# Softmax denominators of both halves of the heads in one tile, turned once for 512 queries

## The chip, the core and the metric

The kernel runs on one core of one Trainium2 chip. The metric is the time on the device in microseconds. Before the change it was 3248.77 us, the median of three runs (3247.61 to 3251.02).

## The reference

A graph attention layer with residuals and layer norms works on 8 frames of 2048 nodes with 256 channels each. There are 8 heads of 32 channels. All data are fp32. The adjacency matrix is the same for all frames.

```python
qkv = jnp.einsum('fnc,ck->fnk', x, w_qkv)
scores = jnp.einsum('fnhd,fmhd->fhnm', q, k) / jnp.sqrt(jnp.asarray(D, x.dtype))
scores = jnp.where(mask, scores, jnp.asarray(-1000000000.0, x.dtype))
attn = jax.nn.softmax(scores, axis=-1)
t = jnp.einsum('fhnm,fmhd->fnhd', attn, v).reshape(F, N, C)
x = _layernorm(x + t, ln1_g, ln1_b)
h = jax.nn.relu(jnp.einsum('fnc,cd->fnd', x, w1) + b1)
f_out = jnp.einsum('fnd,dc->fnc', h, w2) + b2
x = _layernorm(x + f_out, ln2_g, ln2_b)
```

Around it stands one more residual and norm: the output is the layer norm of the input plus this layer's result. The kernel doesn't subtract a maximum before the exponential. It computes exponentials, sums them for each head and query (the denominators), and divides at the end. It also keeps a running sum and minimum of the denominators (RS); if they are out of range, another, slower path recomputes everything. That path isn't taken here.

## The kernel before

**Tiles and items.** The queries of a frame are cut in 4 chunks of 512 (qc), the heads in 2 halves of 4 (g), the keys in 16 blocks of 128 (mb). An item is (frame, qc, g, mb). There are 8 x 4 x 2 x 16 = 1024 items, 128 to a frame, and the main loop (L552) goes through them in this order. Scores are computed with keys on the partitions and queries along the free dimension: an item is a tile p of 128 keys by 4 heads by 512 queries.

**What an item does.** Four matmuls on TensorE, in different rows of its array, make the scores in two PSUM pairs of banks (L230). VectorE (DVE) adds the mask to each pair and writes it into p (L233). ScalarE (ACT) takes the exponential of p in place (L237). TensorE multiplies with the values into a PSUM bank that holds for all 16 blocks (L249). Scores are two items ahead of the values, exponentials one. The three score pairs rotate, so that scores of an item need that the first mask add of the item before it is done.

**Denominators.** Sums over the keys are first made elementwise over the 16 blocks of a group (f, qc, g). GpSimd (POOL) adds seven of them (POOLED, L271), two chains of four are added by DMAs that accumulate (MOVED, L268, issued on POOL's queue), and one stays alone. That leaves four terms. `denominator` multiplies each with 32 columns of ones, for each head into the 32 partitions of this head (L310), so that a PSUM bank holds the sum of each head, 32 times over, for 512 queries. ACT copies it to dT (L312). TensorE turns dT by four 128x128 transposes (L95, in `transposes`), and DVE takes the reciprocals of one column in 32 into rc (L321) and updates RS (L322, L323). It does this twice for each chunk of queries, once for each half of the heads.

**What follows for a chunk.** After the second half `outcome` starts: `divide` turns the two value tiles oT, DVE multiplies by rc (L345), and a DMA adds the input (L334). `tail` normalizes (`norm`: DVE statistics L278 and L279, four small POOL steps L282 to L286, ACT's L289), goes through the feed-forward (`feed_forward`: L409 to L436, with POOL's L412 and L414), normalizes, scales on POOL (L355, L357), adds the input by a DMA (L359), normalizes again, and stores.

**What sets the order.** The engines work through their own queues in the order in which the program writes them, and a planner in the program writes this order. Besides the main loop there is a list `fill` of generators: denominators, outcomes, tails, and the projections and turned inputs of the next frame (`NEXT`, L499). Once an item, `advance` lets them write some work, ordered by due time. A `yield` tells what a generator needs: a number is a pause in items, BANK the one PSUM bank that the fillers share, MORE the right to another unit in the same bank, WAIT a wait until an item. TensorE's filling is limited by credit: 2200 for each item, not saved up, of which a unit of four 512-column matmuls takes 2048 and a set of four transposes 1400 (TURN). Another unit starts only with 1024 left, or when the filler is overdue. These lines decide it:

```python
state["credit"] = min(max(state["credit"], 0) + STEP, KEPT)
...
return finish or state["credit"] >= UNIT or min(due) <= t
```

A denominator is started two items after its group ends and is due six items after that; its last term waits until the fourth item after the group's end. What the fillers write on DVE, ACT and POOL in an item stands ahead of the mask adds, the exponential and the pool add that the main loop writes next.

## Time and profile before

One execution was profiled. It took 3242.05 us, 6.7 less than the median of the three runs; its span, from the first to the last instruction, is 3240.0 us, at a mean granted TensorE clock of 0.987.

| Engine | busy, us | share of the span |
|---|---|---|
| TensorE matmuls (PE) | 3101.0 | 96% |
| VectorE (DVE) | 2739.5 | 85% |
| GpSimd (POOL) | 2593.3 | 80% |
| ScalarE (ACT) | 2435.5 | 75% |

The costliest groups are DVE's mask adds (2410.5 us), ACT's exponentials (1956.3), POOL's adds (1829.5), and TensorE's scores (1171.2), values (1092.9) and denominators (261.1 for the terms, 47.3 for the turns of dT).

A group's line of the profile gives the source line, engine, operation, output and inputs with their shapes, and the count; then the busy time and the mean duration of one in ns; then how long the engine idled just before them, and what ended that. A timeline's line gives start and duration in us, engine, line, operation, tiles, count, and in brackets the idle time before it with what ended it. TensorE carries out an fp32 matmul as two records, so four matmuls are eight. Records of one engine can overlap: the next begins before the last one's end is written. The chain that ended last goes back from the last instruction to whatever released each step.

### The profile page before, as it was taken

The page shows a single profiled execution, that of the slowest core. Times are in us where ns is not written, and L with a number is a line of the kernel's source. Part 1 is how long each engine was busy: PE and PEld are TensorE (multiplying, and loading weights), DVE is VectorE, ACT ScalarE, POOL GpSimd, SP SyncE. Part 2 cuts the span into 40 slices and gives each one's busy share as a digit, 9 for nine tenths or more (in the row PEclk, how much of TensorE's full clock was granted, in tenths as well). Part 3 has the DMA queues.
Part 4 walks back from the last instruction along what each step waited for, and adds up shares of the span by engine and source line. Part 5 has one row for each costly group of instructions (what it writes and reads, how often), then busy time and mean ns, then how long its engine had stood idle before and what let it go on. Part 6 is the DMA issues. An engine that isn't in the chain of part 4 may idle for free.

```text
span 3240.0 us, 68306 instructions
## 1 busy us (share of the span) xinstructions
PE 3101.0 (96%) x28948; PEld 976.0 (30%) x28948; DVE 2739.5 (85%) x3203; ACT 2435.5 (75%) x1937; POOL 2593.3 (80%) x1357
## 2 busy tenths in 40 slices
PE   7899999999999999999999999999999999998994
PEld 4222333323332233322333323323233323332221
DVE  4888888888888888888988888888888888888994
ACT  3667778778778777778777778777778777777773
POOL 0568888788878888788887888888888788878894
PEclk8899999999999999999999999999999999999997
DMA  9688779778879788788788879878788878877773
GB/s 322 147 179 190 182 175 202 176 174 200 181 176 205 171 190 193 158 195 200 177 181 175 184 181 220 177 167 197 175 192 194 180 171 201 181 171 160 168 160 78
DMA packets 153384, 591.57 MB, mean 183 GB/s; under 512 B 15056, under 2 KB 67792, under 8 KB 103920
## 3 DMA queue, kind: packets, MB, share of 16 engines
q0 software_dynamic: 64560, 435.85, 67.2%
q1 hardware_dynamic: 87696, 149.98, 13.1%
q8 instruction: 229, 3.75, 0.4%
q10 hardware_dynamic: 816, 1.31, 0.1%
q14 instruction: 83, 0.68, 0.1%
HBM read 146.67 MB, written 37.75 MB: 57 GB/s over the span
## 4 chain that ended last, share of the span: by engine, by line
PE 75%; DVE 8%; POOL 5%; DMA 4%; issue 4%; ACT 2%; DVEq 0%; ACTq 0%; POOLq 0%
PE s L230 28%; PE x L249 24%; PE x L54 13%; DVE p L233 6%; PE x L310 6%; PE x L95 4%; DMA p<-p 3%; POOL p L271 2%; ACT p L237 2%; DMA mask<-md 1%; POOL y L357 1%; DVE st L278 1%; POOL y L355 0%; POOL y L414 0%; POOL y L412 0%
## 5 line engine op out<-in xcount | busy, mean ns | idle before, releaser
L233 DVE TENSOR_TENSOR p<-s,mask 128x1024 f32<-128x1024 f32 x2048 | 2410.5, 1219 | 360.3 <-PE s L230 202.9
L237 ACT ACTIVATE p<-p 128x2048 f32<-128x2048 f32 x1024 | 1956.3, 1910 | 510.2 <-DVE p L233 456.7
L271 POOL TENSOR_TENSOR p<-p 128x2048 f32<-128x2048 f32 x382 | 1829.5, 4791 | 216.0 <-ACT p L237 213.8
L230 PE MATMUL s<-qT,kT 32*128 32x512 f32 x8192 | 1171.2, 641 | 34.1 <-DVE p L233 29.1
L249 PE MATMUL x<-p,v 128*32 128x512 f32 x8192 | 1092.9, 606 | 16.7 <-ACT p L237 16.7
L268 POOL DMA_DIRECT2D p<-p x384 | 360.1, 957 | 305.5 <-ACT p L237 95.5
L230 PEld LDWEIGHTS s<-qT,kT 32*128 32x128 f32 x8192 | 320.5, 183 | 637.8 <-DVE p L233 580.1
L249 PEld LDWEIGHTS x<-p,v 128*32 128x32 f32 x8192 | 161.3, 108 | 796.4 <-issue 302.6
L310 PE MATMUL x<-p,ones 128*32 128x512 f32 x2016 | 261.1, 594 | 15.9 <-POOL p L271 9.7
L289 ACT ACTIVATE y<-y,nb,rs 128x256 f32<-128x256 f32 x372 | 219.2, 590 | 46.1 <-POOL nb L286 46.1
L54 PE MATMUL x<-in,wqkv 128*32 128x512 f32 x1888 | 243.5, 592 | 0.0
L278 DVE BATCH_NORM_STATS2 st<-y 128x6 f32<-128x256 f32 x372 | 155.2, 417 | 6.2 <-DMA y<-in_x_dram 6.2
L54 PE MATMUL x<-w2s,hT 128*32 128x256 f32 x2048 | 122.8, 381 | 3.3 <-DVE y L436 2.3
L54 PE MATMUL x<-turned,w1s 128*32 128x512 f32 x992 | 122.9, 592 | 0.4 <-ACT in L166 0.4
L54 PEld LDWEIGHTS x<-wqkv,in 128*32 128x32 f32 x3584 | 102.2, 110 | 63.5 <-issue 59.0
L54 PE MATMUL x<-wqkv,in 128*32 128x128 f32 x3584 | 117.2, 273 | 0.0
L310 PEld LDWEIGHTS x<-p,ones 128*32 128x32 f32 x2016 | 64.1, 110 | 171.4 <-issue 136.0
L54 PEld LDWEIGHTS x<-in,wqkv 128*32 128x32 f32 x1888 | 61.7, 110 | 140.9 <-issue 113.7
L283 POOL TENSOR_TENSOR rs<-rs,mhalf 128x4 f32<-128x4 f32 x93 | 97.1, 1044 | 7.7
L54 PEld LDWEIGHTS x<-w2s,hT 128*32 128x32 f32 x2048 | 66.1, 110 | 76.5 <-issue 30.3
L414 POOL TENSOR_TENSOR y<-y,be1b2r 128x1024 f32<-128x1024 f32 x32 | 85.4, 2667 | 0.6
L355 POOL TENSOR_TENSOR y<-y,g2r 128x1024 f32<-128x1024 f32 x31 | 82.7, 2668 | 1.2 <-ACT y L289 1.2
(117 smaller groups left out, 1333.1 us busy)
## 6 DMA issues: line engine op xcount, KB each, us to landing
p<-p POOLq DMA_DIRECT2D x384, 1024.0 KB, 10.5
in<-xd SPq DMA_DIRECT2D x87, 512.0 KB, 10.7
mask<-md SPq DMA_DIRECT2D x248, 128.0 KB, 8.0
y<-in_x_dram POOLq DMA_DIRECT2D x62, 512.0 KB, 8.0
p<-in_adj_dram SPq DMA_DIRECT2D x16, 1024.0 KB, 9.7
out_dram<-y SPq DMA_DIRECT2D x31, 512.0 KB, 6.4
in<-in_x_dram SPq DMA_DIRECT2D x29, 512.0 KB, 15.9
xd<-in SPq DMA_DIRECT2D x28, 512.0 KB, 10.9
```

The lines of the kernel that those rows point to most:

```text
L54: nc.tensor.matmul(out[r:r + D], lhsT[:, r:r + D], rhs, start=start, stop=stop)
L95: nc.tensor.transpose(ps[:, j * P:(j + 1) * P], s, ident)
L230: nc.tensor.matmul(ps2[half][:, j, :], KT[f, mb // TPC, g][r:r + D, (mb % TPC) * P:(mb % TPC + 1) * P], QT[f, qc, g][r:r + D, :], start=Tr ...
L233: nc.vector.tensor_tensor(pt[:, 2 * half:2 * half + 2, :], ps, MK[f, qc, mb // 2][:, mb % 2, None, :].to_broadcast([P, 2, CH]), ALU.add)
L237: nc.scalar.activation(PT[item], PT[item], AF.Exp, scale=1.0 / math.sqrt(D))
L249: nc.tensor.matmul(O[grp][r:r + D, :], V[f, mb // TPC, g][:, mb % TPC, r:r + D], PT[item][:, h, :], start=(mb == 0), stop=(mb == LAST))
L268: nc.gpsimd.dma_start(PT[f, qc, g, chain[0]], PT.pop(item), accum_op=ALU.add)
L271: nc.gpsimd.tensor_tensor(first, first, PT.pop(item), ALU.add)
L278: nc.vector.bn_stats(st, t[:, j, :])
L283: nc.gpsimd.tensor_tensor(rs, rs, cst["mhalf"], ALU.pow)
L289: nc.scalar.activation(t[:, j, :], t[:, j, :], AF.Identity, bias=nb[:, j:j + 1], scale=rs[:, j:j + 1])
L310: nc.tensor.matmul(ps[r:r + D, :], cst["ones"], term[:, h, :], start=(n == 0), stop=(n == len(terms) - 1))
```

## The change

Instead of 32 columns of ones, the weights of the terms now have ones in only half of the 32 columns: the first 16 for the first half of the heads, the last 16 for the second. The other columns are zero. The first half's sums are copied to dT by ACT as before, and its denominator ends there. The second half's sums are added to dT by DVE, straight from PSUM. The tile then holds, for each position of a head in its half, 16 partitions of the first half's sum and 16 of the second's, and is turned once. The reciprocal takes one column in 16, for all 8 heads; rc now has the halves alternating, and `divide` reads it with a step of two. RS has twice the width. Three memsets make the new weights.

```diff
             for h in range(4):
                 r = D * h
-                nc.tensor.matmul(ps[r:r + D, :], cst["ones"], term[:, h, :], start=(n == 0), stop=(n == len(terms) - 1))
-        dT = op.tile([P, CH], F32, name="dT")
-        nc.scalar.copy(dT, ps)
+                nc.tensor.matmul(ps[r:r + D, :], cst["halves"][:, g, :], term[:, h, :], start=(n == 0), stop=(n == len(terms) - 1))
+        if g == 0:
+            DT[f, qc] = op.tile([P, CH], F32, name="dT")
+            nc.scalar.copy(DT[f, qc], ps)
+            return
+        dT = DT.pop((f, qc))
+        nc.vector.tensor_tensor(dT, ps, dT, ALU.add)
         yield 1
         yield BANK
         ps = bank()
         transposes(ps, [dT[:, j::TPC] for j in range(TPC)])
-        if g == 0:
-            RC[f, qc] = op.tile([P, TPC, H], F32, name="rc")
-        rc = RC[f, qc]
-        den = ps.rearrange("p (j c) -> p j c", c=P)[:, :, ::D]
-        nc.vector.reciprocal(rc[:, :, 4 * g:4 * g + 4], den)
+        rc = RC[f, qc] = op.tile([P, TPC, H], F32, name="rc")
+        den = ps.rearrange("p (j c) -> p j c", c=P)[:, :, ::D // 2]
+        nc.vector.reciprocal(rc, den)
         nc.vector.tensor_tensor(RS[:, 0], RS[:, 0], den, ALU.add)
         nc.vector.tensor_tensor(RS[:, 1], RS[:, 1], den, ALU.min)
-        if g == 1:
-            begin = items.index((f, qc, g, LAST)) + SUM + 2
-            start(begin, outcome(f, qc) if (f, qc) != (F - 1, NCK - 1) else finish(f, qc), begin)
+        begin = items.index((f, qc, g, LAST)) + SUM + 2
+        start(begin, outcome(f, qc) if (f, qc) != (F - 1, NCK - 1) else finish(f, qc), begin)
...
-                                    rc[:, :, 4 * gg:4 * gg + 4, None].to_broadcast([P, TPC, 4, D]), ALU.mult)
+                                    rc[:, :, gg::2, None].to_broadcast([P, TPC, 4, D]), ALU.mult)
...
-    RS = const.tile([P, 2, TPC, H // 2], F32, name="RS")
+    cst["halves"] = const.tile([P, 2, D], F32, name="halves")
+    nc.gpsimd.memset(cst["halves"], 0.0)
+    for g in range(2):
+        nc.gpsimd.memset(cst["halves"][:, g, g * D // 2:(g + 1) * D // 2], 1.0)
+    RS = const.tile([P, 2, TPC, H], F32, name="RS")
```

More of the change, by code (lines that the diff above doesn't have):

```diff
@@ L217, in project @@
         give(xT)
-    PT, O, OT, RC = {}, {}, {}, {}
+    PT, O, OT, RC, DT = {}, {}, {}, {}, {}
     def scores(item):
```

## The prediction

> **What bounds the kernel now.** I read the page's busy shares first, then the chain that ended last:

> ```profile
> PE 3101.0 (96%) x28948; PEld 976.0 (30%) x28948; DVE 2739.5 (85%) x3203; ACT 2435.5 (75%) x1937; POOL 2593.3 (80%) x1357
> ...
> PE 75%; DVE 8%; POOL 5%; DMA 4%; issue 4%; ACT 2%; DVEq 0%; ACTq 0%; POOLq 0%
> ```

> TensorE is busy nearly all the time and carries three quarters of the chain, but POOL, DMA and DVE hold a sixth of it, so both count. For the stages I cut the timeline of TensorE at the first score matmul (L230) of each of the 1024 items and sorted the gaps by what else TensorE does in them. They are very even. Median: 2.54 us with scores and values alone; 2.75 with the turn of dT or oT (L95); 2.66 with the turn of y or an input; 2.93 with one unit of four column matmuls (projection, denominator term, feed-forward); 3.79 with two units. So the turn of a denominator tile costs 0.21 us over an empty step, and a second unit in a step 0.86 over the first. With medians for all steps, frames 2 to 6 would take 382.4 us each; they take 387.1 to 390.2. The rest is a few stalls at the same items of every frame; I number items 0 to 127 within a frame: TensorE's steps by the item scored, POOL's by the item added, two behind.

> Next the groups kept apart by shape, for what is removed and for the nearest thing to what is added:

> ```profile
> L95 PE MATMUL x<-ident,dT 128*128 128x128 f32 x252 | 47.3, 310 | 0.0
> ...
> L436 DVE TENSOR_TENSOR y<-x,y 128x512 f32<-128x512 f32 x64 | 44.2, 691 | 42.5 <-PE x L54 32.6 <-POOL y L414 9.8
> ```

> The timelines of DVE and of TensorE around one second-half denominator (item 70, frame 4) show how tight DVE is there:

> ```profile
> 1847.90 0.42 DVE L278 BATCH_NORM_STATS2 st<-y 128x6 f32<-128x256 f32 x1
> 1848.35 0.18 DVE L279 BATCH_NORM_AGGREGATE mv<-st 128x2 f32<-128x6 f32 x1
> 1848.48 2.36 DVE L233 TENSOR_TENSOR p<-s,mask 128x1024 f32<-128x1024 f32 x2
> ...
> 1854.17 2.35 DVE L233 TENSOR_TENSOR p<-s,mask 128x1024 f32<-128x1024 f32 x2
> ```

> ```profile
> 1847.28 1.14 PE L230 MATMUL s<-qT,kT 32*128 32x512 f32 x8
> ...
> 1850.02 1.14 PE L230 MATMUL s<-qT,kT 32*128 32x512 f32 x8
> ...
> 1855.52 0.71 PE L230 MATMUL s<-qT,kT 32*128 32x512 f32 x4
> ```

> Scores need a PSUM pair that the first of the two mask adds before them has read. That add ends 1.22 us after its start: 1849.70 for the scores at 1850.02, a slack of 0.32; 1855.39 for those at 1855.52, a slack of 0.13.

> POOL's timeline in frame 4 and in frame 7, items 58 to 62, shows a stall and a longer one:

> ```profile
> 1815.40 0.86 POOL L268 DMA_DIRECT2D p<-p  x1 [7.27 <-issue]
> 1815.96 4.88 POOL L271 TENSOR_TENSOR p<-p 128x2048 f32<-128x2048 f32 x1
> ...
> 1822.60 0.19 POOL L286 TENSOR_SCALAR nb<-nb 128x4 f32<-128x4 f32 x1
> ```

> ```profile
> 2978.43 0.86 POOL L268 DMA_DIRECT2D p<-p  x1 [4.57 <-issue]
> 2978.99 2.72 POOL L412 TENSOR_TENSOR y<-y,g1r 128x1024 f32<-128x1024 f32 x1
> 2981.33 4.88 POOL L271 TENSOR_TENSOR p<-p 128x2048 f32<-128x2048 f32 x1
> ...
> 2987.97 0.19 POOL L286 TENSOR_SCALAR nb<-nb 128x4 f32<-128x4 f32 x1
> ```

> A norm's last POOL step (L286) releases L289 on ACT, and the next exponential stands behind L289. ACT idles 3.74 us in frame 4 (the step takes 5.73 instead of 3.79), and 6.91 in frame 7, where L412 stands ahead of the pool add L271 (a step of 10.41 instead of 3.79).

> The last stall is the denominator's own, at items 82 to 85:

> ```profile
> 1887.61 1.06 PE L310 MATMUL x<-p,ones 128*32 128x512 f32 x8 [1.12 <-POOL p L271]
> ```

> Its last term waits for POOL. Over the medians, its steps lose 2.5, 4.6, 1.75, 1.65, 1.7 and 3.1 us in frames 1 to 6.

> [...]

> **The change part by part.**

> *Removed on TensorE.* 32 of 64 turns of dT. A turn also takes a place in the filling order (it uses 1400 of the 2200 credit, and 800 is under a unit), so later units move up and fewer are overdue and doubled. The order of the two built programs gives the steps by content, before and after: one unit 592 and 646, two units 65 and 38, turn of dT 63 and 31, empty 62 and 67, the rest alike (the last item's run-out, with one turn in each, is outside). So 54 x 2.93 - 27 x 3.79 - 32 x 2.75 + 5 x 2.54 = 158.2 - 102.3 - 88.0 + 12.7 = -19.4 us.

> *Added on DVE.* 32 adds of 128x512 (PSUM and SBUF) take the place of ACT copies of 585 ns; ACT has slack there. 31 fall within the loop, and 30 of these stand in a step that also holds a bn_stats and bn_aggr. The add doesn't wait long: the last term's matmuls end by about 1847.4, before DVE is through with its mask adds at 1847.9. But the masks behind it start later. A like record (L345, 0.68) holds the queue for 0.60 (1853.57 to 1854.17); against the smallest slack that follows, 0.13, TensorE loses 0.47: 31 x 0.47 = +14.6. Bounds: 0, if later idle time of DVE absorbs all, and 31 x 0.69 = +21.4. What is late next is the exponential, by the same amount; values come a step later and hide it. The reciprocal and the two RS operations of the first half go (0.24 + 0.11 + 0.16, within steps already counted); those left have 32 instead of 16 elements. I cost that, two more memsets on POOL at the start (about 0.2 us, beside loads) and the strided rc at nothing: were the cover gone, under 1 us.

> *Moved: POOL's queue at items 58 to 62.* In frames 3 to 6 the built order now has L412 (2.35 us) ahead of the pool add and the norm, as frame 7 has before. L289 stays where it was, behind exponential 62, and gets there about 0.3 later: +2.0 in each of 4 frames, +8.2. The bound is frame 7's, 6.6 - 1.8 = 4.8 each, +19; the other is 0. In frames 1 and 2 the norm comes ahead of the pool add, and the stalls of 1.4 and 1.7 should go: -3.1.

> *Moved: denominators.* At items 82 to 85 in frames 2 to 6 query projections go first, so the last term stands one step (2.9 us) later than before, more than POOL was late in most; the norm also goes ahead of the pool add at item 70, and L355 no longer stands behind a waiting DMA issue. These stalls go: -12.9, and frame 1's -2.5 by POOL's order alone. At items 114 to 117 in frames 1 to 6, the last term comes a step earlier: POOL ends its sum 19.3 to 19.7 steps into that group, the term now stands at 19.7, and the chain's DMA (10.5 us to landing) is as close: +2 in all, 0 to +9. The feed-forward's add at item 98 waited for L414 (3.1 over its medians); L414 now goes ahead of a DMA issue: -2.5.

> Sum: -19.4 + 14.6 + 8.2 - 3.1 - 15.4 + 2 - 2.5 = -15.6 us. The profiled execution took 3242.05 (span 3240.0, 2 around it), so it would take 3226.5; the median, 6.7 above it, 3233.

> **The rivals.** *The add is hidden*: without its 14.6, 3219. For: DVE idles 360 us ahead of mask adds. Against: little of that lies in these steps.

> *The stalls move and don't go.* POOL and its DMAs are 80% and 67% busy; TensorE, freed at item 85, meets POOL again at 98 or 117. Without the gains at the stalls (21.0), and with the rest, it is +5.4: 3254 at worst; with two thirds of them lost, about 3247, which I take. For: DMA and POOL hold 9% of the chain. Against: POOL itself idles 1.3, 2.0 and 3.1 us in the group after.

> *Slower: DVE becomes the bound at the second half.* If the add is not 0.47 but drags the following turns (dT, oT, oT, each near DVE's rate) so that a whole mask pair comes late, an event costs more. Without it the sum is -30.2, so it decides from 0.97 us an event; at 1.6 it is +19, 3268. For: three steps in a row with 0.13 to 0.32 of slack. Against: the add itself is 0.69.

> That the change doesn't do what it says is excluded by the built order: 31 turns in the loop instead of 63.

> **How the numbers follow.** The forecast 0.51 (own range 3225 to 3242), hidden add 0.14, moved stalls 0.25, DVE bound 0.10. About 0.2%, 6.5 us, is what a measurement of this kernel can tell from no change. Faster: 0.49 + 0.14 + 0.06 = 0.69; within: 0.02 + 0.18 = 0.20; slower: 0.01 + 0.10 = 0.11. The range 3217 to 3251 leaves out most of the DVE case and the ends of the others.

> **What would show it.** Steps after: some 31 of 2.75 with dT, 38 of 3.79. A DVE line of 32 adds of about 690 ns; scores after it late by half a microsecond. ACT's wait on L286 of about 6 us in frames 3 to 6. No wait of the last term on POOL at item 85. It is wrong if steps with two units stay at 65, if the scores lose over 0.9 after each add, or if waits on POOL or DMA grow at items 98 or 114 to 117.

## The result

The changed kernel takes 3251.45 us (median of 22 runs, 3246.52 to 3260.16), the kernel before 3248.0 in the runs beside it (22 runs, 3239.89 to 3252.86). The ratio is 1.0014, with an interval of 1.0008 to 1.0020: slightly slower, and within the 0.2% that count as no change here. The forecast was 3233. The rival nearest to it is the one called "The stalls move and don't go" (3247).

The profiled execution of the changed kernel took 3250.26 us (span 3248.5, mean granted clock 0.982), that of the kernel before 3242.05 (span 3240.0, clock 0.987). So the two profiles lie 8.2 us apart, and the medians 3.45, because the profile of before was one of its shorter executions. All sums below compare the two profiles.

From the page of the changed kernel, the busy times and the chain that ended last:

```profile
PE 3090.9 (95%) x28820; PEld 961.4 (30%) x28820; DVE 2752.0 (85%) x3139; ACT 2415.2 (74%) x1905; POOL 2591.6 (80%) x1360
...
PE 65%; DVE 14%; POOL 6%; DMA 6%; issue 4%; ACT 2%; DVEq 0%; POOLq 0%; ACTq 0%; SPq 0%
```

TensorE has 10 us less to do, and its share of the chain falls from 75% to 65%; DVE, POOL and DMA together rise from 17% to 26%. The work went, and waiting came. The groups say where, and what for:

```profile
L289 ACT ACTIVATE y<-y,nb,rs 128x256 f32<-128x256 f32 x372 | 219.5, 591 | 55.1 <-POOL nb L286 55.1
L310 PE MATMUL x<-p,halves 128*32 128x512 f32 x2016 | 262.7, 595 | 6.6 <-DMA p<-p 6.5
...
L95 PE MATMUL x<-ident,dT 128*128 128x128 f32 x124 | 23.1, 309 | 0.0
```

Half of the turns of dT are gone (124 records instead of 252). The terms of the denominators wait 6.6 us in all instead of 15.9, and no longer for POOL. But ACT's scaling of the norm (L289) waits 55.1 us for POOL instead of 46.1.

I cut TensorE's timeline into the same steps as for the prediction (from one item's first score matmul to the next one's), and took the excess of each over the median that its content had before. The loop over the 1024 items became 5.7 us longer; the start took 0.6 more and what follows the loop 2.2, which is the 8.5 between the spans. In the first row both columns are counts of steps times the medians of before.

| Part of the loop | predicted, us | measured, us |
|---|---|---|
| steps by their content | -19.4 | -19.4 |
| longer steps at the 31 adds | +14.6 | +8.5 |
| item 65, frames 3 to 6 | +8.2 | +21.1 |
| items 64 and 65, frames 1, 2 and 7 | -3.1 | -3.7 |
| last terms at items 84 to 86 | -15.4 | -13.8 |
| items 114 to 117 | +2 | -0.9 |
| item 98 | -2.5 | -3.1 |
| items 93 and 94, frames 2 to 6 | none | +7.4 |
| item 101, frames 2 to 6 | none | +3.8 |
| items 49 and 50, frame 1 | none | +5.5 |
| all others | none | +0.2 |

**Item 65.** These are POOL's lines in frame 4 of the changed kernel, to be held against those of frame 4 and frame 7 before:

```profile
1812.94 0.85 POOL L268 DMA_DIRECT2D p<-p  x1 [6.58 <-issue]
1813.50 2.69 POOL L413 TENSOR_TENSOR y<-y,g1r 128x1024 f32<-128x1024 f32 x1
1815.85 4.84 POOL L271 TENSOR_TENSOR p<-p 128x2048 f32<-128x2048 f32 x1
...
1822.45 0.19 POOL L286 TENSOR_SCALAR nb<-nb 128x4 f32<-128x4 f32 x1
```

L413 (the old L412) stands ahead of the pool add, as predicted: from the start of the DMA issue to that of L286 it is 9.5 us instead of 7.2. ACT and TensorE of the same moment:

```profile
1822.67 0.60 ACT L289 ACTIVATE y<-y,nb,rs 128x256 f32<-128x256 f32 x1 [5.78 <-POOL nb L286]
```

```profile
1819.86 1.14 PE L230 MATMUL s<-qT,kT 32*128 32x512 f32 x8
1825.13 1.94 PE L249 MATMUL x<-p,v 128*32 128x512 f32 x8 [4.13 <-ACT p L237]
1826.84 2.65 PE L54 MATMUL x<-w2s,hT 128*32 128x256 f32 x32
```

ACT idles 5.78 us instead of 3.74, the predicted two more. TensorE idles 4.13 instead of 1.88. This is TensorE before, at the same item of frame 4 and, in the second pair, of frame 7:

```profile
1825.28 1.06 PE L249 MATMUL x<-p,v 128*32 128x512 f32 x8 [1.88 <-ACT p L237]
1826.16 1.90 PE L54 MATMUL x<-turned,w1s 128*32 128x512 f32 x16
```

```profile
2990.66 1.94 PE L249 MATMUL x<-p,v 128*32 128x512 f32 x8 [5.06 <-ACT p L237]
2992.36 2.57 PE L54 MATMUL x<-w2s,hT 128*32 128x256 f32 x32
```

And then something shows in the changed kernel that the prediction did not have: the value matmuls after the wait take 1.94 us where the same eight records elsewhere take 1.07, and the 32 records of L54 behind them 2.65 instead of 1.91. The profile cut into windows of 2 us gives the reason. The columns are the window, its length, and the busy time of TensorE, its weight loads, DVE, ACT and POOL with the number of instructions; then the granted TensorE clock, the share of the DMA engines, and GB/s. First the changed kernel, then the one before in the window behind its own wait:

```profile
1824.00:1826.00 2.00, 0.87 (x7) 0.20 (x8) 0.00 (x0) 2.00 (x3) 2.00 (x3) 0.73 0.07 17
1826.00:1828.00 2.00, 2.00 (x20) 0.74 (x16) 0.00 (x0) 2.00 (x3) 2.00 (x1) 0.50 0.98 197
1828.00:1830.00 2.00, 2.00 (x32) 0.87 (x24) 0.37 (x1) 2.00 (x3) 2.00 (x1) 0.92 0.96 197
```

```profile
1826.00:1828.00 2.00, 2.00 (x22) 0.40 (x14) 0.00 (x0) 2.00 (x3) 2.00 (x1) 1.00 1.00 213
```

After the wait of 4.13 us TensorE is granted 0.50 of its clock for 3.41 us; before, after 1.88 us of idling, it stayed at 1.00. I went through both profiles in windows of 1 us, and added up TensorE's busy time times (1 - clock): within the loop, from 110 us on, it is 4.8 us before, in three places, and 15.9 after, in eight. Item 65 of frames 3 to 6 has 1.9, 1.6, 2.8 and 2.0 of it, 8.3 together; before, these four had none. TensorE's idle time there is 4.89, 4.13, 4.72 and 6.10, together 19.8 (before 6.6). Idle time and clock give the 28.0 us that the four steps lose, against 6.9 before.

**The denominators.** Around item 70 in frame 4, DVE:

```profile
1845.52 0.68 DVE L316 TENSOR_TENSOR dT<-x,dT 128x512 f32<-128x512 f32 x1
1846.11 0.42 DVE L278 BATCH_NORM_STATS2 st<-y 128x6 f32<-128x256 f32 x1
...
1846.66 2.33 DVE L233 TENSOR_TENSOR p<-s,mask 128x1024 f32<-128x1024 f32 x2
```

and TensorE:

```profile
1847.92 1.14 PE L230 MATMUL s<-qT,kT 32*128 32x512 f32 x8 [0.21 <-DVE p L233]
```

The add holds DVE's queue for 0.59 us, as estimated, and the scores wait for the mask add. But TensorE loses only 0.21 to this wait, and the steps with a turn of dT have a median of 3.02 instead of 2.75. At items 83 to 86 of frame 4 the last of the four terms waits for nothing, where that of before waited 1.12:

```profile
1889.81 1.04 PE L310 MATMUL x<-p,halves 128*32 128x512 f32 x8
```

**New waits.** Three lines of the changed kernel, one of ACT (item 93, frame 4), one of DVE (item 101, frame 4) and one of TensorE (item 49, frame 1):

```profile
1909.63 0.60 ACT L289 ACTIVATE y<-y,nb,rs 128x256 f32<-128x256 f32 x1 [2.16 <-POOL nb L286]
```

```profile
1936.28 2.35 DVE L233 TENSOR_TENSOR p<-s,mask 128x1024 f32<-128x1024 f32 x2 [1.07 <-DMA p<-p]
```

```profile
616.78 1.12 PE L95 MATMUL x<-ident,in 128*128 128x128 f32 x4 [3.93 <-DMA in<-in_x_dram]
```

The first is the same wait as at item 65, for the second norm of the chunk. The second is a mask add that waits 1.07 us for a DMA that reads its tile p. The third is the load of an input. The first and the third are followed by the half clock too (0.50 for 3.41 us in frames 5 and 1, which takes 1.6 us each).

### The profile page after: what moved, and what is told of

Read it like the earlier page. It is cut to its first block, busy times and chain, and to the rows that moved or that the text cites. A ratio compares the mean times of both kernels' runs of the same rounds, so it can differ in the third digit from the quotient of the medians.

```text
span 3248.5 us, 68003 instructions
## 1 busy us (share of the span) xinstructions
PE 3090.9 (95%) x28820; PEld 961.4 (30%) x28820; DVE 2752.0 (85%) x3139; ACT 2415.2 (74%) x1905; POOL 2591.6 (80%) x1360
## 3 DMA queue, kind: packets, MB, share of 16 engines
q1 hardware_dynamic: 87696, 149.98, 13.4%
q8 instruction: 228, 3.74, 0.4%
## 4 chain that ended last, share of the span: by engine, by line
PE 65%; DVE 14%; POOL 6%; DMA 6%; issue 4%; ACT 2%; DVEq 0%; POOLq 0%; ACTq 0%; SPq 0%
PE s L230 24%; PE x L249 21%; PE x L54 14%; DVE p L233 11%; DMA p<-p 5%; PE x L310 3%; POOL p L271 3%; PE x L95 3%; DVE st L278 1%; ACT p L237 1%; POOL y L413 1%; POOL rs L283 1%; DVE dT L316 1%; POOL y L358 1%; DMA in<-in_x_dram 1%
## 5 line engine op out<-in xcount | busy, mean ns | idle before, releaser
L233 DVE TENSOR_TENSOR p<-s,mask 128x1024 f32<-128x1024 f32 x2048 | 2408.9, 1218 | 331.4 <-PE s L230 170.0
L271 POOL TENSOR_TENSOR p<-p 128x2048 f32<-128x2048 f32 x382 | 1829.9, 4790 | 223.0 <-ACT p L237 220.3
L230 PE MATMUL s<-qT,kT 32*128 32x512 f32 x8192 | 1172.0, 642 | 44.0 <-DVE p L233 39.5
L268 POOL DMA_DIRECT2D p<-p x384 | 358.2, 951 | 278.5 <-ACT p L237 123.1
L230 PEld LDWEIGHTS s<-qT,kT 32*128 32x128 f32 x8192 | 321.0, 183 | 674.0 <-DVE p L233 637.3
L310 PE MATMUL x<-p,halves 128*32 128x512 f32 x2016 | 262.7, 595 | 6.6 <-DMA p<-p 6.5
L289 ACT ACTIVATE y<-y,nb,rs 128x256 f32<-128x256 f32 x372 | 219.5, 591 | 55.1 <-POOL nb L286 55.1
L54 PE MATMUL x<-in,wqkv 128*32 128x512 f32 x1888 | 245.7, 592 | 0.0
L278 DVE BATCH_NORM_STATS2 st<-y 128x6 f32<-128x256 f32 x372 | 155.0, 417 | 5.7 <-DMA y<-in_x_dram 5.7
L54 PE MATMUL x<-turned,w1s 128*32 128x512 f32 x992 | 125.0, 596 | 5.9 <-ACT in L166 5.9
L54 PE MATMUL x<-w2s,hT 128*32 128x256 f32 x2048 | 127.2, 391 | 1.1 <-ACT oT L253 0.7
L54 PEld LDWEIGHTS x<-wqkv,in 128*32 128x32 f32 x3584 | 102.2, 110 | 64.1 <-issue 56.0
L54 PE MATMUL x<-wqkv,in 128*32 128x128 f32 x3584 | 117.4, 273 | 0.0
L310 PEld LDWEIGHTS x<-p,halves 128*32 128x32 f32 x2016 | 65.1, 110 | 160.0 <-issue 141.1
L54 PEld LDWEIGHTS x<-in,wqkv 128*32 128x32 f32 x1888 | 61.3, 110 | 141.3 <-issue 116.6
L437 DVE TENSOR_TENSOR y<-x,y 128x512 f32<-128x512 f32 x64 | 44.2, 691 | 63.3 <-PE x L54 61.8
L54 PEld LDWEIGHTS x<-w2s,hT 128*32 128x32 f32 x2048 | 68.0, 113 | 78.7 <-issue 39.9
L413 POOL TENSOR_TENSOR y<-y,g1r 128x1024 f32<-128x1024 f32 x32 | 84.3, 2634 | 0.1
## 6 DMA issues: line engine op xcount, KB each, us to landing
in<-xd SPq DMA_DIRECT2D x87, 512.0 KB, 10.1
```

The source lines that it names most:

```text
L54: nc.tensor.matmul(out[r:r + D], lhsT[:, r:r + D], rhs, start=start, stop=stop)
L230: nc.tensor.matmul(ps2[half][:, j, :], KT[f, mb // TPC, g][r:r + D, (mb % TPC) * P:(mb % TPC + 1) * P], QT[f, qc, g][r:r + D, :], start=Tr ...
L233: nc.vector.tensor_tensor(pt[:, 2 * half:2 * half + 2, :], ps, MK[f, qc, mb // 2][:, mb % 2, None, :].to_broadcast([P, 2, CH]), ALU.add)
L268: nc.gpsimd.dma_start(PT[f, qc, g, chain[0]], PT.pop(item), accum_op=ALU.add)
L271: nc.gpsimd.tensor_tensor(first, first, PT.pop(item), ALU.add)
L278: nc.vector.bn_stats(st, t[:, j, :])
```

## The experiments

Two theories stood at first. One: what eats the gain is ACT, held at L289 by a norm that is late in POOL's queue; what counts is POOL's order. The other: TensorE, once it has less to do, meets the other engines somewhere anyway, and what is gained at one place is given back at the next. Each change of POOL's order below leaves the order of every other engine as it was.

**1. The changed kernel, with L413 one item later in the first tail of frames 3 to 6**, so behind the pool add and the norm, as before the change.

```diff
-        yield from feed_forward(y)
+        yield from feed_forward(y, late=qc == 0 and 3 <= f <= 6)
...
         yield 1
-        nc.gpsimd.tensor_tensor(y, y, rows(cst["g1r"]), ALU.mult)
+        if not late:
+            nc.gpsimd.tensor_tensor(y, y, rows(cst["g1r"]), ALU.mult)
         yield 1
+        if late:
+            nc.gpsimd.tensor_tensor(y, y, rows(cst["g1r"]), ALU.mult)
```

> The changed kernel, but in the first tail of frames 3 to 6 POOL's multiply by g1 (L413 in the profile after) is written one item later, behind the pool add and the norm, as the kernel before had it. TensorE, DVE and ACT keep their orders. Theory A (POOL's queue order holds ACT's norm and with it the exponential at item 65): the stalls at items 64 and 65 of these frames, 28.0 us over the medians in the profile after, fall to 7 to 10, and the time goes from 3251 to about 3232. Theory B (POOL and its DMAs are the limit, stalls only move): as much comes back at items 85 to 101, and the time stays at 3246 to 3252.

Measured: 3241.29 us (12 runs), beside 3246.7 for the kernel before; ratio 0.998, 0.9972 to 0.9989. Against the changed kernel's 1.0014 that is about 11 us gained. The four steps of item 65 lose 13.4 us instead of 28.0 (0.4, 4.2, 3.7 and 5.2), and ACT idles 1.75, 4.19, 3.54 and 5.42 there. So POOL's order is a large part of it. It is not all: before, the same four lose 6.9. The larger part of the remainder is the clock. TensorE's idle time is 8.2 us here (6.6 before), but in three of the four frames the half clock follows, and takes 4.6 more. The profile of this run (3246.14 us) is one of its longer executions: in frame 1 TensorE waits 7.4 us for an input, and 10.2 us are lost at items 61 and 62, which the edit doesn't touch.

**2. The kernel before, with the same multiplication one item earlier in the same four places**, so with nothing of the change but this.

```diff
-        yield from feed_forward(y)
+        yield from feed_forward(y, early=qc == 0 and 3 <= f <= 6)
...
+        if early:
+            nc.gpsimd.tensor_tensor(y, y, rows(cst["g1r"]), ALU.mult)
         yield 1
-        nc.gpsimd.tensor_tensor(y, y, rows(cst["g1r"]), ALU.mult)
+        if not early:
+            nc.gpsimd.tensor_tensor(y, y, rows(cst["g1r"]), ALU.mult)
```

> The kernel before, but in the first tail of frames 3 to 6 POOL's multiply by g1 (L412) is written one item earlier, ahead of the pool add and the norm, the order that the change brought. Nothing else moves. Theory A: the stall at item 65 grows from 6.9 us in sum to about 28, and the time from 3248 to about 3269. Theory B: TensorE's later arrival spares it the waits at item 85 (8.0 us in these frames), and the time stays below 3261.

Measured: 3265.69 us (5 runs), ratio 1.0056, 1.0042 to 1.0069, which is 18 us lost. Item 65 of frames 3 to 6 loses 24.4 us instead of 6.9. TensorE's lines in frame 4:

```profile
1834.38 1.93 PE L249 MATMUL x<-p,v 128*32 128x512 f32 x8 [4.30 <-ACT p L237]
1836.09 3.64 PE L54 MATMUL x<-turned,w1s 128*32 128x512 f32 x16
```

The wait and the slow matmuls behind it (3.64 instead of 1.90 before) are there without any denominator being changed: 16.8 of the 24.4 are idle time and 7.5 the clock. The last terms at items 84 to 86 lose no less than before. That a stall of 18 us is taken back later is refuted for this place.

**3. The kernel before, with DVE in ACT's place for the second half's dT**: it adds a column of zeros to the PSUM tile, and the result is the same. This measures the add in place of the copy, without the rest of the change.

```diff
-        nc.scalar.copy(dT, ps)
+        if g == 0:
+            nc.scalar.copy(dT, ps)
+        else:
+            nc.vector.tensor_tensor(dT, ps, cst["zeros"].to_broadcast([P, CH]), ALU.add)
...
+    cst["zeros"] = const.tile([P, 1], F32, name="zeros")
+    nc.gpsimd.memset(cst["zeros"], 0.0)
```

> The kernel before, but the copy of the second half's sums to dT (32 of 64 ACT copies) is an add on DVE of the PSUM bank and zeros; orders are otherwise kept. It prices the added DVE operation alone. By the profile after, where the step with the turn of dT is 0.26 us over its median of before: 31 x 0.26 = +8, 3256. By the prediction's 0.47 each: +14.6, 3263. If DVE's idle time hides it: 3248.

Measured: 3249.83 us (13 runs) beside 3246.7; ratio 1.0004, 0.9996 to 1.0012. By the medians the adds cost 3 us, by the ratio 1, with an interval from -1 to +4, so in the time they can't be told from nothing. In the steps it is 0.27 each; all turns of dT together lose 6.8 us instead of 0.9, while the stalls at items 84 to 86 lose 4.5 less than before. The prediction had 14.6.

**4. The changed kernel in the order of before.** The first half's denominator takes its old place in the filling order and its credit, though it turns nothing.

```diff
             nc.scalar.copy(DT[f, qc], ps)
+            yield 1
+            yield BANK
+            state["credit"] -= TURN
             return
```

> The changed kernel with its operations, but the first half's denominator keeps its place in the filling (a pause, the bank, the 1400 of credit) without turning anything, so that everything else stands in the order of the kernel before: 32 steps go from a turn to an empty one. Theory A (the order of the fillers is what cost the gain): 32 x -0.21 = -6.7 for the steps, +8 for the adds, stalls at items 65 and 85 as before: 3249, within 3 us. If instead the operations themselves cost what the change lost: 3255 or more. Theory B says nothing apart here.

Measured: 3247.31 us (13 runs), ratio 1.000, 0.9991 to 1.0008. Turns that go without their places being filled are worth 32 times 0.21 = 6.7 us by the medians, the steps with the adds lose 6.6, and nothing is left. What the change gains and loses beyond that comes with the places that other work moves into. The stalls of items 84 to 86 are halved here (7.5 us instead of 15.4) although nothing stands elsewhere on TensorE, and items 93 to 95 lose 7.9 instead of 1.1: a part of the stalls does move on. Item 65 of frames 3 to 6 loses 11.3 us instead of 6.9 even in the old order, 3.4 of it by the clock.

**5. The changed kernel, with the whole feed-forward of the first tail in frames 3 to 6 an item later**, to see whether the place of its matmuls beside item 65 is the cause. Its multiplication by g1 then stands behind the norm again too.

```diff
-        yield from feed_forward(y)
+        yield from feed_forward(y, late=qc == 0 and 3 <= f <= 6)
...
         state["turned"] = True
+        if late:
+            yield 1
```

> The changed kernel, but the feed-forward of the first tail in frames 3 to 6 waits one item more, so that its steps stand at items 59 to 67 as in the kernel before: at item 65 TensorE has the second matmuls with w1 (W1) again instead of the first with w2 (W2), and POOL's multiply by g1 comes after the norm by itself. Theory A1 (at item 65 the loss is larger than ACT's idle time explains by before's ratio because W2 waits for an hT that stands on ACT behind the held norm): the stall there goes back to about 7 us in sum for these frames, 21 us under the 28.0 of the profile after and 6 under what moving the multiply alone leaves (13.4): 3231 to 3236. Rival A2 (the place of W2 doesn't matter, the pool add's lateness does): as with the multiply alone, 13 us there and 3239 to 3243. Theory B (stalls only move): 3246 or more.

Measured: 3252.27 us (14 runs), ratio 1.0016, 1.0007 to 1.0024: as the changed kernel. Item 65 itself loses only 4.7 us in frames 3 to 6 (13.4 in run 1, where the multiplication alone was moved). But items 61 to 67 of these frames still lose about 20 us together: in three of the four, an input now comes late, and items 62 and 63 lose 14.4. In frame 5:

```profile
2203.80 1.08 PE L95 MATMUL x<-ident,in 128*128 128x128 f32 x4 [5.78 <-DMA in<-in_x_dram]
2204.81 2.09 PE L230 MATMUL s<-qT,kT 32*128 32x512 f32 x8
```

So this run doesn't settle what part the place of the feed-forward's matmuls has at item 65; moving everything picked another wait, here again with scores behind it that take 2.09 us instead of 1.14.

**6 and 7. The norm's small POOL steps an item earlier**, ahead of whatever POOL has to write in the item after the statistics; L289 stays where it is. Run 6 is the changed kernel with it, run 7 the kernel before.

```diff
             nc.vector.bn_aggr(mv[:, j, :], st)
-            yield 1
+            if j < TPC - 1:
+                yield 1
...
-        yield 2
+        yield 3
         for j in range(TPC):
             nc.scalar.activation(t[:, j, :], t[:, j, :], AF.Identity, bias=nb[:, j:j + 1], scale=rs[:, j:j + 1])
```

> The changed kernel; in every norm the four small POOL steps are written one item earlier, ahead of the pool add or DMA issue of that item, and ACT's part stays where it is. TensorE, DVE and ACT keep their orders. Theory A (ACT held by norms behind pool adds): the stalls at items 65 (33 us in sum in frames 3 to 7) and 93 (8) fall to 10 together, and the time goes from 3251 to about 3222. Theory B (POOL is the limit): POOL now also waits for DVE's statistics, its adds end later, the last denominator terms wait instead at items 85 and 101, and the time is 3240 or more.

> The kernel before with the same edit of the norms. Theory A: the stall at item 65 (16.6 us in sum) goes, those at items 85 (15.4) stay: 3233. Against it the changed kernel with the same edit shows what the change is worth when the norm no longer holds ACT: by the steps -18.9, by the adds +3 to +8, by the stalls at items 85 and 98 up to -17: 10 or more faster. Theory B: 3245 or more, and no difference between the two with the edit.

Measured on the same chip: run 6 takes 3230.91 us (5 runs, 3230.44 to 3232.14), ratio to before 0.9948, 0.9935 to 0.9962. Run 7 takes 3256.9 (9 runs), ratio 1.0031, 1.0021 to 1.0041. With the norm first, the change is worth 26 us; without it, it costs some 4. Run 6 is faster than both kernels that were compared. Its POOL in frame 4:

```profile
1811.33 0.86 POOL L268 DMA_DIRECT2D p<-p  x1 [5.90 <-issue]
...
1813.94 0.19 POOL L287 TENSOR_SCALAR nb<-nb 128x4 f32<-128x4 f32 x1
1814.10 2.41 POOL L414 TENSOR_TENSOR y<-y,g1r 128x1024 f32<-128x1024 f32 x1
1816.45 4.60 POOL L271 TENSOR_TENSOR p<-p 128x2048 f32<-128x2048 f32 x1
```

The last step of the norm comes 2.6 us after the DMA issue instead of 9.5, since the two long operations follow it. ACT's idle time ahead of its scaling falls from 55.1 to 13.4 us in the whole kernel, the stalls at item 93 are gone, and items 64 to 66 lose about 11 us in all frames together instead of 34. The half clock costs 3.3 us in the loop instead of 15.9.

In run 7 ACT waits as little (10.1 us), and yet the kernel gets slower. Its TensorE in frame 4, at item 85:

```profile
1894.14 1.06 PE L311 MATMUL x<-p,ones 128*32 128x512 f32 x8 [3.43 <-DMA p<-p]
1895.13 2.01 PE L230 MATMUL s<-qT,kT 32*128 32x512 f32 x8
```

The stalls at items 84 to 86 have grown from about 15 to about 34 us, and the clock takes its share again (12.8 us in the loop). In frame 4 the chain's last DMA is issued 0.9 us after the start of item 82, where in the kernel before it was issued 3.6 us ahead of it, and it takes 10.8 us to land. POOL idles 7.5 us ahead of this issue, so POOL's queue is not what holds it. It is issued 0.5 us after the DMA ahead of it in its chain has landed, and that one took 15.0 us instead of 11.4 (in the other frames 13.4 to 14.9 instead of 11.5 to 12.9). So most of the 4.5 us comes from a DMA that takes longer; why it does was not settled. So in the kernel before, what is gained at item 65 is lost again at items 84 to 86, as the second theory has it. With the change, the denominator's last term stands an item later, those items give little back (3.0 us in run 6, 1.6 without its edit), and the gain stays, as the first has it. Which part the later term has in this, apart from the rest of the change, was not tried by itself.

**8. The changed kernel, with TensorE kept busy in the wait of item 65.** The fall of the clock was seen only beside the waits so far. Here the scores of item 65 are written five times in frames 3 to 6, with the same values.

```diff
-        for half in (1, 0):
+        for half in (1, 0) * (5 if 3 <= f <= 6 and (qc, g, mb) == (2, 0, 1) else 1):
```

> This kernel is the changed one; TensorE only writes the scores of item 65 in frames 3 to 6 five times over instead of once, each time the same values, so that it works through most of the stretch (4.89, 4.13, 4.72 and 6.10 us in the profile of after) in which it stands waiting for the exponential of item 63. Nothing else is moved. Once takes 1.07 us, four more take 4.28, which leaves TensorE idle for 0.6, 0, 0.4 and 1.8 us. Item 65 loses 28.0 us in the profile of after: 19.8 idle and 8.3 because the granted clock falls to about a half for some microseconds after the idle stretch. Theory C, the clock falls because TensorE stood idle: no fall of the granted clock at 1435, 1825, 2215 and 2609 us, the four steps lose 20 to 21 us instead of 28, and the kernel takes about 8 us less than the changed one, 3243. Rival D, the clock falls for another reason (the kind of work that follows, or a rhythm of its own): it falls there all the same, the four steps lose 28 or more, and the time stays at 3251 or somewhat above. The extra work costs nothing in either, since the exponential decides when the values start.

Measured: 3239.19 us (9 runs), ratio to before 0.9972, 0.9960 to 0.9985, so 12 to 14 us less than the changed kernel, with 17 us more work for TensorE. The lines of frame 4, and one of its windows:

```profile
1819.46 4.57 PE L230 MATMUL s<-qT,kT 32*128 32x512 f32 x40
1823.97 1.07 PE L249 MATMUL x<-p,v 128*32 128x512 f32 x8
1824.85 1.91 PE L54 MATMUL x<-w2s,hT 128*32 128x256 f32 x32
```

```profile
1824.00:1826.00 2.00, 2.00 (x36) 0.97 (x36) 1.82 (x2) 2.00 (x3) 2.00 (x2) 1.00 0.64 131
```

No idle time ahead of the values, no fall of the clock (1.00), and the matmuls behind take what they take elsewhere. The clock's loss in the loop goes from 15.9 to 6.5 us: the 8.3 that item 65 had are gone, and the 1.6 at item 93 of frame 5. So at item 65 the clock fell because TensorE stood still for 4.1 to 6.1 us. The four steps lose 14.6 us (4.3, 3.4, 3.4 and 3.4) instead of the 20 that this theory expected: ACT waits only 5.6, 4.7, 4.2 and 4.7 us here instead of 6.5, 5.8, 6.4 and 7.8. A TensorE that doesn't lose time in one frame meets POOL in another phase in the next; which part of that does it was not taken apart.

## Why the prediction was wrong, step by step

*What was right.* The medians carried over: the counts of steps came out as built, and the steps without an add or a stall take after what they took before. The stalls of the last terms went as said (-13.8 for -15.4; the 1.6 between are a stall that stayed in frame 1), those of item 98 too (-3.1 for -2.5). The two stalls at item 65 of frames 1 and 2 went as said (-3.1). That their row comes to -3.7 is luck: a stall of 1.3 came at item 64 of frame 2, and frame 7, which wasn't counted, lost 1.9 less. Items 114 to 117, for which 2 were set aside, cost nothing, and the 0.9 lost there before went. POOL's order at items 58 to 62 was read rightly, and so was where ACT would stand for it. One reading, without consequence, was too wide: that an fp32 matmul is two records holds for the scores (8192 for 1024 items of four), but a transpose of dT is one (252 in 63 sets of four, 310 ns each in the mean).

*The step that failed most* is "+2.0 in each of 4 frames, +8.2". It came out at +21.1, above the 19 that was given as its bound. Two things were wrong in it. First its size: 2.0 was right for frame 4, whose ACT idled 2.04 more, but frames 3, 5 and 6 idled 2.5, 3.7 and 4.1 more, 12.4 in all. TensorE's idle time grew with it by 13.2. Second, the working priced a wait by its length alone. The bound was taken from frame 7, whose step holds both idle time and half clock (5.06 us and 1.5), and from frame 4, whose step holds no fall; the prediction took their difference, 4.8, for a delay. The waits of before, 0.85 to 2.14 us, were not followed by a fall, and those after, 4.1 to 6.1, were. Run 8 keeps TensorE busy in these waits, and the 8.3 us are gone. The profile of before had the evidence: behind the wait of 5.06 us in frame 7 (shown above) the value matmuls take 1.94 us and the 32 records of L54 2.57, instead of 1.06 and 1.91.

*The second* is the price of new and returned stalls. Only items 114 to 117 were named; what came was items 93 and 94 (+7.4), 101 (+3.8) and the input in frame 1 (+5.5), 16.7 together. That the stalls would partly move was a rival with 0.25, and it was kept apart from the forecast although it needs nothing that contradicts it. Runs 4 and 7 show returns of this kind. That item 93 is POOL's order again is shown by run 6, where it is gone; the loss at item 101 stays in run 6 and grows (8.8 us), and why it comes there was not settled. The input of frame 1, and the 2.2 us after the loop, were not looked into.

*The third* is the add, mis-sized in the other direction: 0.47 us each, +14.6. The step's reasoning was right in kind, since scores wait for the mask add behind it. But it set the add's 0.60 against the smallest slack of the steps that follow, 0.13. The step with the turn of dT had the other one, 0.32, and 0.60 - 0.32 = 0.28 is what the steps show, 0.27; the later steps lost next to nothing more (the turns of oT 1.3 us in all). In time, run 3 gives 1 to 3 us, within its noise. By that time the lower rival ("The add is hidden") was nearer; by the 8.5 of the steps, the forecast was. The DVE rival, which needed 0.97 each, is excluded.

Together: +12.9 at item 65, +16.7 of new waits, -6.1 at the adds, and the small rest come to the 24 us between -15.6 and the +8.2 of the two profiles.

## What to carry to other kernels

When a change moves work in a queue, look for short steps there that release another engine, and put them ahead of the long ones: putting four small POOL operations ahead of two long ones took some 20 us off the changed kernel (run 6), about what the change saved in TensorE's steps. Try such a reordering together with the change, as without it it was a loss of 10 (run 7). And read the granted clock behind each wait of TensorE: in these profiles a wait that grew past some 2 us could cost 1.3 to 3.1 us more than its length.

## What the runs showed of the hardware

In the ten profiles of this study I took every idle stretch of TensorE of 0.8 us or more within the loop, from 110 us on, and the clock granted in the microseconds behind it. Of 77 stretches up to 1.85 us none is followed by a fall. Of 37 between 1.85 and 3.28 us, 22 are. Of 30 longer ones, all are.

```profile
623.50:626.91 3.41, 1.55 (x20) 0.32 (x16) 2.78 (x5) 2.41 (x2) 3.11 (x3) 1.00 0.45 107
626.91:630.32 3.41, 3.41 (x20) 0.72 (x16) 0.22 (x1) 1.41 (x1) 3.41 (x1) 0.50 0.83 129
```

```profile
2990.97:2994.39 3.42, 1.77 (x16) 0.31 (x8) 2.84 (x4) 0.83 (x2) 3.08 (x6) 1.00 0.26 53
2994.39:2997.80 3.41, 1.79 (x28) 0.84 (x32) 0.85 (x1) 3.41 (x4) 3.41 (x3) 1.00 0.19 38
2997.80:3001.21 3.41, 3.41 (x48) 1.30 (x44) 1.91 (x3) 3.41 (x4) 3.41 (x1) 1.00 1.14 231
```

A fall took 1.3 to 3.1 us, with a median of 1.7, counted as TensorE's busy time in it times (1 - clock). The windows ahead of the falls were not all idle throughout: 55% of idle time is the least among them, and the shortest wait that a fall followed is the one of 1.86 us.
